# A graph-attention layer on one core: the first head's weights on SyncE's queue, and one step of transposes moved

## The chip, the cores and the metric

The kernel runs on one core of a Trainium2 chip. A core has five engines that run side by side, each through its own list of instructions in order: TensorE (PE; its weight loads are listed apart as PEld), VectorE (DVE), ScalarE (ACT), GpSimd (POOL) and SyncE (SP), which here only issues transfers. They wait for each other by semaphores. Transfers between the chip's memory and the core's are issued by SyncE, ScalarE or GpSimd into a queue of that engine, and 16 DMA engines carry them out.

The metric is the device time of one execution in microseconds (us). Times of single instructions come from the trace of one profiled execution and count from its start.

## The reference, cut to what matters

The input x has 128 graphs of 64 nodes with 512 features; all graphs share one adjacency matrix. Everything is 32-bit floating point.

```python
h = relu(layernorm(x))
# four heads, each with its own W (512x512) and a (2x512)
Wh   = einsum('bnf,hfo->bhno', h, W_heads)
f1, f2 = Wh @ a[:, :512], Wh @ a[:, 512:]
e    = leaky_relu(f1[..., :, None] + f2[..., None, :], 0.01)
attn = softmax(where(adj > 0, e, -1e9))
h    = elu(attn @ Wh)                # heads side by side: 2048 features
# the same once more with W_out (2048x512) and a_out, one head
out  = elu(gat(h, W_out, a_out))
y    = relu(out @ w1 + b1) @ w2 + b2 + out
return x + layernorm(y) * gamma + beta
```

## The kernel before, in words

The 8192 rows of x are 64 tiles of 128 rows (two graphs each), and four tiles make a group `g`; there are 16 groups. The large products are done by a scheme with seven products of half-size blocks instead of eight (`unit`, L242), so the kernel also makes sums of weight blocks: `weight_sums` (L193) makes them on GpSimd and writes them to memory as `tc`, and `piece` (L211) loads a block of weights or of such sums as a tile `w` over SyncE's queue whenever one of 11 places becomes free.

The steps are written out in the order in which they are to be issued. A scheduler then places each instruction in the list of its engine, and a tile's place is reused as soon as its last reader is done. `behind(ins, after, ...)` (L86) adds a wait of one instruction for another by hand.

**The start** (L97 to L201 and L856 to L881) is different from the rest. The first four tiles of x are loaded by `load` (L104) on SyncE's queue. ScalarE loads the vectors `a` into `ar`, a tile that VectorE cleared before (`zeros`, L113). `fetch` (L163) loads the weights of a head, 512x512, as `pw`: head 0 on ScalarE's queue, behind `zeros`; heads 1 to 3 on SyncE's queue, the later matrices on GpSimd's. Then:

- `norm1` (L339) normalizes a tile: statistics on VectorE (L326, L330, L332), the reciprocal root and bias on GpSimd (L334, L344), relu with scale and bias on ScalarE (L346), which gives `hn`. For the first four tiles the GpSimd parts are chained one behind the other.
- `transpose_h` (L359) turns `hn` on PE (`pth`, L362); ScalarE copies it to `hT`.
- `spread_a` (L171) spreads the vectors `a` of a head over 128 rows by two matmuls on PE (`pab`, L177). `fold` (L183) multiplies the head's weights by them and sums, eight instructions on VectorE per head (`jk`, L188), 32 for the four heads; the results `wa` go into `project_f` (`pf`, L372), from which the scores come.
- `head_w(m, j)` (L626) is the product of tile j with head m's weights on PE (`hw`, L629); ScalarE copies it out (L632). In the list of PE the first of them stands behind the spreads of heads 0 and 1 and the transposes of tile 0.
- `weight_sums(0)` on GpSimd (L200 to L205) reads `pw` of head 0 behind the last bias of the four tiles.

Group 0's first layer is done in this way; from group 1 on `attend1` and `project1` do it in the other order with the blocks of seven products.

**The step at group 0's second layer** (L973 to L997). `project2(0)` is a list of 28 products of blocks (`g_b`, L305: seven products of four parts each). Between its steps stands a table by step number with other work: at 15 to 21 the transposes, scores and softmax of group 2 (`softmax`, L414, whose result is the tile `s1A`, L443 and L448), at 25 `turns[1]` and at 27 `turns[4]`. Each of these two is `transpose_weights` (L473) for a pair of tiles: eight transposes on PE into two banks (`s1pt`, L485), and two copies on ScalarE to `at` (L489). The banks come from a pool of two; `s1A` has one place, so the softmax of the second pair writes its result there after the first pair's transposes have read it. The steps of the next `project1` follow.

Of the kernel before, what the change touches and what calls it, by code (L numbers as in the profile page):

```python
# [9 lines left out]
FP = mybir.dt.float32  # L10
# [12 lines left out]
def gat_preln_kernel(  # L23
# [30 lines left out]
    nc = tc.nc  # L54
    P = 128
    B, N, F = x.shape
    H = W_heads.shape[0]
# [6 lines left out]
    G = 4  # L64
# [4 lines left out]
    xf = x.rearrange("b n f -> (b n) f")  # L69
    of = out.rearrange("b n f -> (b n) f")  # L70
# [4 lines left out]
    wk = ctx.enter_context(tc.tile_pool(name="wk", bufs=2))  # L75
# [10 lines left out]
    def behind(ins, after, reason):  # L86
        tc.add_manual_dep(
            ins.ins, after.ins.name,
            mybir.DependencyInfo(mybir.DependencyClass.Sync, mybir.DependencyReason.DATA),
            reason=reason,  # L90
        )
# [9 lines left out]

    X, HN, HNS, AT = {}, {}, {}, {}

    def load(t, name="x"):  # L104

        tl = wk.tile([P, F], FP, tag="x", name=f"{name}{t}", bufs=4)
        nc.sync.dma_start(out=tl, in_=xf[ts(t, P), :])
        return tl

    X[0] = load(0)  # L110
# [1 line left out]
    ar = wk.tile([P, O], FP, tag="elu", name="ar", bufs=3)  # L112
    zeros = nc.vector.memset(ar, 0.0)  # L113
    nc.scalar.dma_start(out=ar[0:2 * H], in_=a_heads.rearrange("h (r p) -> (h r) p", p=O))
    for t in range(1, G):
        X[t] = load(t)
    aj = const.tile([P, N], mybir.dt.int32, name="aj")
    for b in range(NB):
        nc.gpsimd.dma_start(out=aj[ts(b, N), :], in_=adj)
# [42 lines left out]

    def fetch(m, after=None):  # L163
        MT[m] = big.tile([P, KC, O], FP, tag=homes[m], name=f"pw{m}")
        queue = nc.scalar if m == 0 else nc.sync if m < H else nc.gpsimd
        ins = queue.dma_start(out=MT[m], in_=mats[m].rearrange("(k p) o -> p k o", p=P))
        if after is not None:
            behind(ins, after, "not in front of what is needed first")
        return ins
# [59 lines left out]
    def flush_late():  # L229
        while late:  # L230
            late.pop(0)()

    def run(steps, side=()):

        side, done = list(side), 0
        for i, fn in enumerate(steps):
            fn()
            while done * len(steps) < (i + 1) * len(side):
                side[done]()
                done += 1  # L240
# [229 lines left out]
    def attn_weights(p):  # L470
        A1[p] = softmax(E1.pop(p), None, 2 * H, "s1", p)
# [23 lines left out]
    def stage_a(g):  # L495


        if g >= NG:
            return [], [], []
        p, r = 2 * g, 2 * g + 1  # L500

        def norms(p):
            norm1(2 * p)
            norm1(2 * p + 1)
            if p >= 2:
                ahead = 2 * p + (4 if p < 4 else 2)
                prefetch(ahead)
                prefetch(ahead + 1)

        def transposes(p):  # L510
            transpose_h(2 * p)
            transpose_h(2 * p + 1)

        return (
            [lambda: norms(p), lambda: norms(r)],
            [
                lambda: transposes(p), lambda: transposes(r), nothing, lambda: project_f(g), nothing,
                lambda: (scores1(g), attn_weights(p)), nothing, lambda: attn_weights(r),
            ],
            [nothing, lambda: transpose_weights(p), nothing, nothing, lambda: transpose_weights(r)],  # L520
        )
# [66 lines left out]
    def project1(g, h):  # L588


        z = ZB[g]
        if h == 0:
            new_h1(g)
        sums = {6: 0, 7: 1, 3: 2}
        blk = {1: "11", 2: "12", 4: "22", 5: "S1"}

        def post(what, a, b=None, to=None):
            if what[0] != "c":
                return
            nm = {"c11": "11", "c12": "12", "c21": "S1", "c22": "22"}[what]  # L600
            dst = H1[nm][:, h]
            if b is not None:
                nc.vector.tensor_tensor(to, a, b, ALU.add)  # L603
                a = to
            elu(flat(dst), flat(a), f"{what}_{g}_{h}")
            if what == "c21":
                nc.gpsimd.tensor_tensor(dst, dst, H1["22"][:, h], ALU.add)  # L607

        s = unit(
            f"a{g}_{h}", product_t(h, lambda p: ZSUM[h][sums[p]] if p in sums else z[blk[p]][:, h]),  # L610
            post, (1, 5, 6, 2, 3, 7, 4),
        )

        def next_sums():
            if h + 1 < H:
                z_sums(g, h + 1)

        return [
            s[0], lambda: (s[1](), flush_late()), lambda: (s[2](), next_sums()), s[3], s[4],
            lambda: (s[5](), late.append(s[6])),  # L620
        ]
# [84 lines left out]
    def scores2(g, j):  # L706
        if j == 0:
            F2[g] = sm.tile([P, 2, G], FP, tag="f2", name=f"f2_{g}")
        f = F2[g]
        for c in range(2):  # L710
            junk = wk.tile([P, FO], FP, tag="elu", name=f"jf{g}_{j}_{c}", bufs=3)
            nc.vector.scalar_tensor_tensor(
                junk, WH2[g][:, j], 1.0, ao[:, c, :], ALU.mult, ALU.mult,
                accum_out=f[:, c, j:j + 1],
            )
# [45 lines left out]
    def stage_e(g):  # L761

        gap = [lambda: None]
        score = [lambda j=j: scores2(g, j) for j in range(G)]
        attend = [lambda q=q: attend2(g, q) for q in range(2)]
        return (
            gap + score + [lambda: spread2(g)] + gap * 2 + [lambda: softmax2(g)] + gap * 5
            + [lambda: transpose_weights2(g)] + gap * 2 + attend[0:1] + gap * 2 + attend[1:2] + gap * 4
        )
# [83 lines left out]
        return [fn for _, _, fn in sorted(keyed, key=lambda k: k[:2])]  # L853


    for m in range(H):  # L856
        fetch(m, zeros if m == 0 else None)
    nc.vector.memset(wa, 0.0)
    norm1(0)
    ab = spread_a(0)  # L860
# [6 lines left out]
    norms, scores, turns = stage_a(1)  # L867
# [77 lines left out]
    for g in range(NG):  # L945
        if g >= 1:
            side = stage_e(g - 1)
            done, n = 0, 6 * H
            for i in range(n):
                if i % 6 == 0:  # L950
                    steps = project1(g, i // 6)
                steps[i % 6]()
                while done * n < (i + 1) * len(side):
                    side[done]()
                    done += 1
            flush_late()
        attn = attend1(g + 1) if g + 1 < NG else []
        norms, scores, turns = stage_a(g + 2)
        tr, ff, fin = feed_forward(g - 1) if g >= 1 else ([], [], [])
        if g == NG - 1:  # L960
            run(project2(g), tr + [nothing] * 6 + ff[:2])
            run(ff[2:], [
                lambda: [scores2(g, j) for j in range(G)], lambda: spread2(g), nothing, nothing,
                lambda: softmax2(g), *[nothing] * 7, lambda: transpose_weights2(g), nothing,
                *[lambda q=q: attend2(g, q) for q in range(2)], nothing,
            ])
            continue
        early = [lambda: z_sums(g + 1, 0)] if g else []
        first = mix(attn, tr, [nothing] * len(attn))
        if g >= 1:  # L970
            first[5:5] = norms[:1]
            first[10:10] = norms[1:]
        if g == 0:  # L973
            side = {
                0: lambda: (attend0(2, 1), turn0(1, 1), project_f(1)),
                1: lambda: (attend0(3, 1), turn0(2, 1)),
                2: lambda: (turn0(3, 1), scores1(1), attn_weights(2), attn_weights(3)),
                5: lambda: weight_sums(M1, LAST["pe"]),
                7: turns1[1],
                8: lambda: fetch(M2, LAST["pe"]),  # L980
                9: attn[0],
                10: lambda: (attn[1](), norms[0](), turns1[4]()),
                12: attn[2],
                13: lambda: (attn[3](), norms[1]()),
                15: scores[0],
                16: scores[1],
                17: lambda: weight_sums(M2, LAST["pe"]),
                18: scores[3],
                20: scores[5],
                21: scores[7],  # L990
                22: lambda: z_sums(g + 1, 0),
                25: turns[1],
                27: lambda: (turns[4](), load_rows()),
            }
            for i, fn in enumerate(project2(g)):
                fn()
                side.get(i, nothing)()  # L997
        else:
            run(project2(g), first + mix(
                ff[:7] + early + ff[7:12] + fin[:1] + ff[12:13] + fin[1:2] + ff[13:],  # L1000
                scores + [nothing] * 8,
            ) + mix(fin[2:], [nothing] + turns + [nothing] * 2))
# [32 lines left out]
```

## Time and profile before

| | |
|---|---|
| median of 4 runs | 2296.99 us |
| the runs | 2297.03, 2296.76, 2297.91, 2296.95 us |
| the profiled execution's own time | 2297.03 us |
| its span, first to last instruction | 2295.0 us |
| mean granted clock of TensorE | 0.998 |
| DMA, mean over the span | 157 GB/s, 361.15 MB |

How to read the lines. A row of the timeline has the start in us, the length in us, the engine, the line of the kernel, the operation, the tile written and the tiles read, the shape and a count; the brackets at the end give the idle time of the engine just before and what ended it. SPq, ACTq and POOLq are the instructions of an engine that issue transfers; their length is that of the issue, not of the transfer. A list of waits has total, number and longest. A row for a stretch of time has, from the left, its bounds and length, the busy time of PE, PEld, DVE, ACT and POOL with the number of instructions, TensorE's granted clock, the share of the DMA engines and GB/s. Matmuls overlap: one starts before the one ahead of it has ended, and their ends are modelled. Tile numbers are left out of names, so `pw` and `hw` stand for all heads.

### The profile page before, as it was taken

How to read it: one execution, taken by the hardware profiler on the slowest of the kernel's cores; microseconds unless marked ns; L12 is line 12 of the kernel's file. 1: busy time of each engine (PE TensorE's matmuls, PEld its weight loads, DVE VectorE, ACT ScalarE, POOL GpSimd, SP SyncE). 2: the span in 40 equal slices, each digit the busy share in tenths (PEclk: the TensorE clock that was granted, in tenths of full speed). 3: DMA queues.
4: the chain of work that ended last, by engine and by line, in shares of the span. 5: the costliest groups of instructions: out<-in, count | busy, mean ns of one | idle time of the engine just before them, and what ended most of it. 6: DMA issues, size and time to landing. Idle time of an engine off the chain costs nothing. (4 is left out here: it accounts for less than half of the span.)

```text
span 2295.0 us, 33254 instructions
## 1 busy us (share of the span) xinstructions
PE 2274.6 (99%) x11856; PEld 1890.7 (82%) x11856; DVE 1275.1 (56%) x2227; ACT 904.4 (39%) x1633; POOL 1018.9 (44%) x906
## 2 busy tenths in 40 slices
PE   9999999999999999999999999999999999999997
PEld 4688888888888888888888888888888888888885
DVE  7555554755546555564655546555465554744427
ACT  3535244252542525335253352534425244251512
POOL 7653524444254442634425344353443525533324
PEclk9999999999999999999999999999999999999999
DMA  7553453534545444453544545345354453635443
GB/s 284 194 183 131 147 179 133 182 131 145 176 134 184 137 151 163 136 184 131 165 152 138 184 133 178 130 147 179 132 181 133 143 178 132 183 118 168 162 147 106
DMA packets 255012, 361.15 MB, mean 157 GB/s; under 512 B 23768, under 2 KB 143608, under 8 KB 254848
## 3 DMA queue, kind: packets, MB, share of 16 engines
q1 hardware_dynamic: 249568, 340.88, 46.1%
q0 software_dynamic: 4576, 16.81, 2.0%
q8 instruction: 96, 1.57, 0.3%
q10 hardware_dynamic: 704, 1.33, 0.2%
q14 instruction: 68, 0.56, 0.1%
HBM read 331.66 MB, written 27.26 MB: 156 GB/s over the span
## 5 line engine op out<-in xcount | busy, mean ns | idle before, releaser
L305 PE MATMUL g_b<-w,h 128*128 128x256 f32 x2560 | 593.1, 379 | 0.0
L305 PEld LDWEIGHTS g_b<-w,h 128*128 128x128 f32 x2560 | 481.1, 190 | 64.6 <-issue 2.0
L289 PE MATMUL g_a<-z,w 128*128 128x256 f32 x1440 | 341.7, 380 | 0.0
L289 PE MATMUL g_a<-zs_z,w 128*128 128x256 f32 x1440 | 336.0, 381 | 0.0
L289 PEld LDWEIGHTS g_a<-zs_z,w 128*128 128x128 f32 x1440 | 269.9, 190 | 59.2 <-issue 24.3
L289 PEld LDWEIGHTS g_a<-z,w 128*128 128x128 f32 x1440 | 272.3, 190 | 41.3 <-DVE g_a L603 5.0
L607 POOL TENSOR_TENSOR hS<-hS,h 128x512 f32<-128x512 f32 x60 | 78.1, 1302 | 360.6 <-DVE hS L573 360.6
L305 PE MATMUL g_b<-w,hS 128*128 128x256 f32 x1024 | 238.2, 379 | 0.0
L305 PEld LDWEIGHTS g_b<-w,hS 128*128 128x128 f32 x1024 | 192.1, 190 | 25.0 <-issue 0.2
L571 ACT ACTIVATE exc<-g_a 128x512 f32<-128x512 f32 x240 | 142.5, 594 | 164.9 <-DVE g_a L603 97.1
L573 DVE SCALAR_TENSOR_TENSOR h<-exc,g_a 128x512 f32<-128x512 f32 x180 | 123.5, 686 | 140.8 <-ACT exc L572 140.2
L572 ACT ACTIVATE exc<-exc 128x512 f32<-128x512 f32 x240 | 151.4, 631 | 6.6
L688 POOL TENSOR_TENSOR h<-h,h 128x512 f32<-128x512 f32 x64 | 86.8, 1365 | 138.6 <-PE g_b L305 138.6
L688 POOL TENSOR_TENSOR h<-hS,h 128x512 f32<-128x512 f32 x64 | 81.5, 1275 | 145.6 <-PE g_b L305 145.3
L314 POOL TENSOR_TENSOR zs_z<-zS,z 128x512 f32<-128x512 f32 x60 | 85.2, 1420 | 136.1 <-PE g_a L289 132.9
L489 ACT COPY at<-s1pt 128x512 f32<-128x512 f32 x64 | 34.4, 589 | 268.8 <-PE s1pt L485 268.8
L833 POOL TENSOR_TENSOR xr<-xr,bs 128x512 f32<-128x512 f32 x64 | 97.5, 1528 | 77.2 <-DMA xr<-in_x_dram 41.3
L305 PE MATMUL g_d<-w,rt 128*128 128x256 f32 x512 | 121.8, 380 | 2.2 <-DVE o L825 1.0
L289 PE MATMUL g_c<-ot,w 128*128 128x256 f32 x512 | 122.7, 382 | 0.6 <-DVE ot L792 0.6
L289 PE MATMUL g_a<-zS,w 128*128 128x256 f32 x480 | 113.4, 379 | 0.0
L305 PEld LDWEIGHTS g_d<-w,rt 128*128 128x128 f32 x512 | 96.9, 190 | 17.3 <-DVE o L825 2.2
L289 PEld LDWEIGHTS g_c<-ot,w 128*128 128x128 f32 x512 | 94.9, 190 | 18.2 <-issue 5.0
(164 smaller groups left out, 3536.0 us busy)
## 6 DMA issues: line engine op xcount, KB each, us to landing
w<-tc SPq DMA_DIRECT2D x624, 256.0 KB, 2.6
w<-in_L_gnn_W_out_dram SPq DMA_DIRECT2D x192, 256.0 KB, 2.7
w<-in_L_gnn_W_heads_dram SPq DMA_DIRECT2D x180, 256.0 KB, 2.9
w<-in_L_gnn_w_dram SPq DMA_DIRECT2D x96, 256.0 KB, 2.7
x<-in_x_dram SPq DMA_DIRECT2D x64, 256.0 KB, 3.2
xr<-in_x_dram SPq DMA_DIRECT2D x128, 128.0 KB, 2.7
out_dram<-o SPq DMA_DIRECT2D x126, 128.0 KB, 2.4
tc<-pt POOLq DMA_DIRECT2D x20, 512.0 KB, 4.3
```

The source lines that it names most:

```text
L289: LAST["pe"] = nc.tensor.matmul(bk[:, o, :], w[:, k, ts(o, P)], a[:, k, :], start=start and o == 0 and k == 0, stop=k == 1, skip_group_che ...
L305: LAST["pe"] = nc.tensor.matmul(bk[:, j, :], a[:, k, ts(j, P)], w[:, k, :], start=start and n == 0, stop=i == len(ms) - 1 and k == 1, skip ...
L314: eng.tensor_tensor(s2, s1, a11, ALU.subtract)
L489: nc.scalar.copy(AT[t].rearrange("p b h n -> p (b h) n"), pt)
L571: nc.scalar.activation(ex, src, AF.Relu, scale=-1.0)
L572: nc.scalar.activation(ex, ex, AF.Exp, scale=-1.0)
L573: nc.vector.scalar_tensor_tensor(dst, ex, -1.0, src, ALU.add, ALU.max)
L607: nc.gpsimd.tensor_tensor(dst, dst, H1["22"][:, h], ALU.add)
L688: nc.gpsimd.tensor_tensor(dst[:, h], x0[:, h], x1[:, h], ALU.subtract)
L833: nc.gpsimd.tensor_tensor(xr, xr, bs, ALU.add)
```

## The change

It has two parts.

1. `fetch(0)` goes to SyncE's queue, behind `zeros` as before, and is written ahead of the loads of tiles 1 to 3 of x, which now wait for `zeros` too. SyncE's list begins with x0, pw of head 0, x1, x2, x3, pw of heads 1, 2, 3. ScalarE's queue has only `ar` at the start. On VectorE the small instruction L332 of tile 0 now stands ahead of the statistics of tile 1, where it stood behind them; two others of tiles 2 and 3 change places. The later loads of x5 to x7 come ahead of the first block of W_out on SyncE's queue.
2. `turns[1]` moves from step 25 to step 26 of the table: in PE's list four matmuls of `project2(0)` come ahead of its eight transposes, and no other order changes.

```diff
-    def load(t, name="x"):
+    def load(t, after=None):
 
-        tl = wk.tile([P, F], FP, tag="x", name=f"{name}{t}", bufs=4)
-        nc.sync.dma_start(out=tl, in_=xf[ts(t, P), :])
+        tl = wk.tile([P, F], FP, tag="x", name=f"x{t}", bufs=4)
+        ins = nc.sync.dma_start(out=tl, in_=xf[ts(t, P), :])
+        if after is not None:
+            behind(ins, after, "not in front of what is needed first")
         return tl
...
-    for t in range(1, G):
-        X[t] = load(t)
...
-        queue = nc.scalar if m == 0 else nc.sync if m < H else nc.gpsimd
+        queue = nc.sync if m < H else nc.gpsimd
...
-    for m in range(H):
-        fetch(m, zeros if m == 0 else None)
+    fetch(0, zeros)
+    for t in range(1, G):
+        X[t] = load(t, after=zeros)
+    for m in range(1, H):
+        fetch(m)
...
-                25: turns[1],
+                26: turns[1],
```

## The prediction

> **What bounds the kernel now.** I read the page first: busy shares, then TensorE's own list of waits, then the timeline of the two places that the change touches. The page says which engine sets the time.
>
> ```profile
> PE 2274.6 (99%) x11856; PEld 1890.7 (82%) x11856; DVE 1275.1 (56%) x2227; ACT 904.4 (39%) x1633; POOL 1018.9 (44%) x906
> ```
>
> TensorE (PE) is busy for 2274.6 of 2295.0 us. The other engines have half their time free, so the end is set by the work of PE, which the change leaves alone, and by its idle time, 20.4 us in all. The list of PE's waits over the whole span says what is in that:
>
> ```profile
> PE pab L177 <- DVE n1st L326: 4.3, 1, 4.3
> PE g_c L289 <- ACT t_c L255: 1.1, 1, 1.1
> ...
> PE hw L629 <- DMA pw<-in_L_gnn_W_heads_dram: 0.9, 1, 0.9
> ...
> PE s1pt L485 <- DVE s1A L443: 0.4, 1, 0.4
> ```
>
> The columns are the total, the number and the longest. Two of them lie where the change works: 0.9 us for the first head's weights (pw), and 0.4 us at the transposes of attention weights (s1pt). No other wait stands between 12 us and 300 us, so a microsecond won on PE at the start is still there at the end: the long tail follows PE. The change can win about 1.3 us by these two rows and no more, 0.06% of the time. A difference of under 0.2% (4.6 us) is what I call no change here; about that much a measurement of this kernel can tell.
>
> **Part 1, the first head's weights.** In order of time, PE at the start (start, length, engine, line):
>
> ```profile
> 4.30 3.75 PE L177 MATMUL pab<-ar,ident 128*128 128x512 f32 x4 [4.30 <-DVE n1st L326]
> 7.85 1.06 PE L362 MATMUL pth<-ident,hn 128*128 128x128 f32 x4
> 8.70 2.68 PE L177 MATMUL pab<-ar,ident 128*128 128x512 f32 x4
> 12.25 3.67 PE L629 MATMUL hw<-pw,hT 128*128 128x512 f32 x8 [0.87 <-DMA pw<-in_L_gnn_W_heads_dram]
> ...
> 17.92 3.60 PE L629 MATMUL hw<-pw,hT 128*128 128x512 f32 x8
> ```
>
> PE finishes the second spread of `a` and waits for pw until 12.25. The last of those matmuls starts at 10.79. Undisturbed ones of this shape follow each other every (3.60 - 0.59) / 7 = 0.43 us (the group at 17.92, less one matmul's own 0.59), so the product could have started at 10.79 + 0.43 = 11.22. It starts 1.03 later, and its group takes 3.67 where the undisturbed one takes 3.60: another 0.07 for starting from a standstill. The wait costs 1.03 + 0.07 = 1.10 us, a little more than the 0.87 that the row names. It goes entirely if pw lands before 11.2.
>
> When does it land? Today it is issued by ScalarE at 2.04 and lands 10.1 us later, at 12.15. The queues at that time:
>
> ```profile
> 0.73 1.81 SPq L107 DMA_DIRECT2D x<-in_x_dram  x4
> ...
> 2.04 0.44 ACTq L166 DMA_DIRECT2D pw<-in_L_gnn_W_heads_dram  x1
> ...
> 2.58 2.24 SPq L166 DMA_DIRECT2D pw<-in_L_gnn_W_heads_dram  x3
> ```
>
> By the trace's times to landing the four tiles of x arrive at 3.5, 4.2, 7.6 and 8.9 us: x2 and x3 slow down as soon as pw runs beside them, and pw shares the 16 engines with x and then with the second head's weights, which land at 13.2. In the changed order everything is on SyncE's queue: x0, pw, x1, x2, x3, then heads 1 to 3. What counts is how many bytes lie ahead. The stretches of the trace give the rate (the last column is GB/s):
>
> ```profile
> 2.00:7.00 5.00, 2.70 (x4) 1.18 (x4) 1.68 (x6) 2.10 (x2) 1.67 (x5) 1.00 0.88 285
> 2.00:9.00 7.00, 4.70 (x9) 2.51 (x10) 2.45 (x9) 2.15 (x3) 2.16 (x6) 1.00 0.91 296
> ```
>
> x0 and pw are 0.26 + 1.05 MB, with the small `ar` and `aj` 1.36 MB: at 285 GB/s that is 4.8 us from 2.0, so 6.8, and with the slowest of the engines lagging I take 7.5. The bounds are 3.5 (not before x0, which is ahead of it) and 12.15 (no sooner than today). 7.5 is near neither, but it has 3.7 us to spare before 11.2, so the term is taken whole: **-1.1 us**.
>
> The Trainium skill, "DMA: Bandwidth & Descriptors", section "Issuing engines are not separate DMA queues", says that queues of several issuing engines run on the same 16 DMA engines and interleave, so that a second issuer saves only issue time. By it the change loses no bandwidth and pw simply moves ahead of x1 to x3; the sum would be the same. The same skill speaks against it in "Perfetto Trace Analysis", section "DMA Optimizations": where issuing itself is the bottleneck, spread it over several engines; this change does the reverse. Weighed by the rows: an issue costs SyncE 1.81 / 4 = 0.45 us, so x1 to x3 are issued one such step (about 0.5 for pw, and 0.2 for its wait) later. By that rule the sum would shrink only if x1 to x3 came too late, which is the next point.
>
> **What the moved load pushes back.** pw now waits for the clearing of `ar` (VectorE, 0.90 to 1.38); x1 to x3 and heads 1 to 3 stand behind it on SyncE. x1 to x3 also have 1 MB more ahead of them: x0 to x3, pw and the small ones are 2.15 MB, at 296 GB/s 7.3 us from 2.0, so x3 lands at about 9.3 instead of 8.9, or 10 with the later issue. Who waits for it? VectorE takes the statistics of x1 to x3 ahead of the first fold, in both kernels:
>
> ```profile
> 8.98 0.69 DVE L326 BATCH_NORM_STATS2 n1st<-x 128x6 f32<-128x512 f32 x1 [0.62 <-DMA x<-in_x_dram]
> ...
> 12.22 0.69 DVE L188 SCALAR_TENSOR_TENSOR jk<-pw,pab 128x512 f32<-128x512 f32 x1 [2.00 <-DMA pw<-in_L_gnn_W_heads_dram]
> ```
>
> From the landing of x3 to VectorE being free for the fold it is 10.22 - 8.93 = 1.3 us. With x3 at 10 the fold starts at 11.3 instead of 12.22: VectorE gains 0.9 us as well. Its 32 folds end 19.5 us later (12.22 to 31.7), and PE needs the last of them at 34.34 today (pf, L372), so at 33.2 after. This holds while x3 lands before 33.2 - 19.5 - 1.3 = 12.4. ScalarE's copy of the first product stands behind hn3, which ends 3.9 us after x3's landing (12.87 against 8.93); PE wants that copy at about 17, which gives nearly the same bound. GpSimd starts its weight sums behind x3's bias, 12.02 today, so perhaps 0.5 to 1 us later; it has 1.5 us idle at 35 and its last sums for W_out reach SyncE at 88.4, some 15 us before PE reads them (from 104). So the term is **0**, covered by 2.4 us; the far bound is in the rival below.
>
> On the gain side there is nothing more ahead of 11.2: the order on PE is unchanged, the first spread waits for `ar`, whose load stays on ScalarE's queue, and x0 stays first. VectorE's eps instruction for x0 is now ahead of x1's statistics and hn0 may be 0.5 us earlier, but the transposes of hn0 follow the spread matmuls without a gap, so that gives nothing.
>
> The cold start is another thing that could blur this: PE's matmuls of 128x512 follow each other every 0.85 us until about 10 and every 0.43 after it. The Trainium skill, "TensorE: Matmul & The Clock Gate", Part 1, says that the array starts at half clock and speeds up after a window of some 3.4 us that runs freely, so that the cold stretch varies from run to run. By that page alone the sum could move by an estimated 1.7 us (3.4 at half speed) either way; the measured spread of the four runs, 1.15 us, is what I use.
>
> **Part 2, the transposes a step later.** The place in the trace:
>
> ```profile
> 156.51 1.04 PE L485 MATMUL s1pt<-ident,s1A 128*128 128x128 f32 x8
> 157.38 3.62 PE L305 MATMUL g_b<-w,h 128*128 128x256 f32 x16
> 160.59 0.69 DVE L443 TENSOR_TENSOR s1A<-s1e,s1r 128x512 f32<-128x512 f32 x1
> 161.43 1.06 PE L485 MATMUL s1pt<-ident,s1A 128*128 128x128 f32 x8 [0.43 <-DVE s1A L443]
> ```
>
> The first eight transposes at 156.51 waited for nothing; the change puts four of the following matmuls (1.73 us) ahead of them. The second eight wait 0.43 us for VectorE's softmax of the second pair. Moving the first eight does not touch that: PE has the same work ahead of 161.0 in another order, and VectorE's chain (exp at 158.53, its sum at 159.57, the product at 160.59) keeps its order. It reuses the tile s1A that the first eight read, but they would end at 159.3, before 160.59. ScalarE copies the first two results at 159.06 behind the exp; they would be ready at 159.3, so the copies end at about 160.4, before PE wants the two banks again at 161.0. The cover shrinks from 0.9 to 0.6 us. So **0**. Bounds: -0.55 (the wait of 0.43 and a restart go) and +1.07 (both copies in front of the second eight); I take 0, since both rows keep their distance.
>
> **Sum.** The profiled execution took 2297.03 us (span 2295.0 and 2.03 around it), 0.04 above the median of the four runs. 2296.99 - 1.10 - 0 = **2295.9 us**.
>
> **Rivals.**
> - *Both waits go* (2295.3): as forecast, and VectorE's softmax reaches PE in time at 161, since VectorE gains as much as PE in front or is less disturbed by GpSimd (its L435 took 1.50 us there, 0.69 elsewhere). Against it: that chain starts from PE's own scores at 146.75, so both shift together. Chance 0.12.
> - *Nothing gained* (2297.0): pw lands late all the same, or PE stops a little later for what was pushed back (x3, or part 2's banks at +1.07). For it: pw's 10.1 us are long. Against it: 3.7 us to spare. Chance 0.10.
> - *Slower: SyncE's queue doesn't carry it alone.* If the one queue ran only at the rate of x2 and x3, 0.52 MB between 4.2 and 8.9, 112 GB/s, the 2.10 MB would take 18.8 us from 2.0: x3 at 20.8, fold at 22.1, end of folds at 41.6 instead of the 33.2 wanted, so PE stands 8.4 us at pf: 2295.9 + 8.4 = 2304.3. It decides from x3 landing after 12.4, a queue below 2.1 / 10.4 = 200 GB/s. Against it: x0 and x1 alone came over this queue by 4.2 us, 0.52 MB in 2.2 us, 238 GB/s. Chance 0.03.
> - *It doesn't do what it says*: the order of the changed program has pw second on SyncE and the eight transposes one product later, so I leave this out.
>
> **Numbers.** Forecast 0.75, then 0.12, 0.10 and 0.03. The range takes in the first three with the runs' spread of about 0.5 either way and part 2's +1.07: 2294.9 to 2297.5. Faster by over 0.2% (below 2292.4) no case gives: 0.01 for what I overlook. Slower by over 0.2% (above 2301.6): 0.03, and 0.01 on top; within: 0.95.
>
> **What would show it.** Right: the product hw starts at 11.2 to 11.3 and PE's list of waits has no row for pw; pw lands at 7 to 8, x3 at 9 to 10; the fold starts ahead of 12; s1pt still waits about 0.4. Wrong: a new wait of PE at hw, pf or pth between 11 and 40 us, or one at s1pt of about a microsecond, or any wait behind it that PE did not have, above all one for weights (w) on SyncE's queue.

## The result, and the profile after

The changed kernel took a median of **2295.15 us** (2293.91 to 2297.04, 41 runs), the kernel before 2297.28 us on the same chips (2295.74 to 2299.12, 61 runs): 2.1 us less, a ratio of 0.999 with a 95% interval of 0.9986 to 0.9995 (1.1 to 3.2 us less). That is inside 0.2%, inside the range, and with the sign that was forecast, but about twice the 1.1 us that the sum named. The profiled execution took 2295.51 us, with a span of 2293.5. Two of the executions behind the medians of this document, 6018.28 us of the kernel before and 8897.45 us of "softmax earlier", lie far above all others; the medians count them and move by at most 0.05 us, the ratios leave them out.

The page's row of busy times after the change: the work of TensorE (PE) is what it was, within a microsecond.

```profile
PE 2273.7 (99%) x11856; PEld 1889.8 (82%) x11856; DVE 1272.5 (55%) x2227; ACT 904.5 (39%) x1633; POOL 1017.3 (44%) x906
```

PE's own list of waits after (total, number, longest):

```profile
PE pab L177 <- DMA ar<-in_L_gnn_a_heads_dram: 3.7, 1, 3.7
PE g_c L289 <- ACT t_c L255: 1.1, 1, 1.1
...
PE hw L629 <- ACT hT L364: 0.9, 1, 0.9
...
PE s1pt L485 <- DVE s1A L443: 0.4, 1, 0.4
```

Three things are to be seen. The row of `hw` for `pw` is gone. A row of `hw` for `hT`, 0.9 us, has come. And the first row, PE's wait before its first matmul, fell from 4.3 to 3.7, which nobody had asked for. The last row, part 2's place, has not moved. (The first wait is put down to VectorE before and to `ar` after. The spread, L177, reads only `ident` and `ar`, so I read both as the wait for `ar`; the profile does not show when `ar` landed.) PE in order of time, after:

```profile
3.67 3.68 PE L177 MATMUL pab<-ar,ident 128*128 128x512 f32 x4 [3.67 <-DMA ar<-in_L_gnn_a_heads_dram]
7.20 0.60 PE L362 MATMUL pth<-ident,hn 128*128 128x128 f32 x4
7.63 1.88 PE L177 MATMUL pab<-ar,ident 128*128 128x512 f32 x4
9.35 3.60 PE L629 MATMUL hw<-pw,hT 128*128 128x512 f32 x8
...
16.20 3.70 PE L629 MATMUL hw<-pw,hT 128*128 128x512 f32 x8 [0.91 <-ACT hT L364]
```

The product of tile 0 starts at 9.35 where it started at 12.25, 2.9 us earlier; that of tile 1 starts at 16.20 where it was 17.92, only 1.7 us earlier. Of what was won, 1.2 us are given back in between. ScalarE shows to whom:

```profile
14.38 0.81 ACT L346 ACTIVATE hn<-x,n1nb,n1rs 128x512 f32<-128x512 f32 x1 [0.18 <-POOL n1nb L344]
15.10 0.56 ACT L632 COPY hw<-hw 128x512 f32<-128x512 f32 x1
15.57 0.58 ACT L364 COPY hT<-pth 128x512 f32<-128x512 f32 x1
```

ScalarE works in order: the copy of tile 1's `hT`, for which PE waits, stands behind the normalization `hn` of tile 3. The normalizations are a chain from VectorE over GpSimd to ScalarE, and the chain of tiles 1 to 3 starts with x1, which now has a megabyte more ahead of it. VectorE gets its statistics of x1 only at 9.40, and its first fold starts at 12.35, no earlier than the 12.22 of before.

```profile
9.40 0.69 DVE L326 BATCH_NORM_STATS2 n1st<-x 128x6 f32<-128x512 f32 x1 [4.64 <-DMA x<-in_x_dram]
...
10.23 0.66 DVE L326 BATCH_NORM_STATS2 n1st<-x 128x6 f32<-128x512 f32 x1
...
10.86 0.68 DVE L326 BATCH_NORM_STATS2 n1st<-x 128x6 f32<-128x512 f32 x1
...
12.35 0.69 DVE L188 SCALAR_TENSOR_TENSOR jk<-pw,pab 128x512 f32<-128x512 f32 x1
```

VectorE waits for x1 alone: its statistics of x2 and x3 follow at 10.23 and 10.86 without a wait. `hn` of tile 3 starts 14.38 - 9.40 = 4.98 us after the statistics of x1; in the other five traces with this order of loads it is 4.97 to 4.99 us, though these statistics start anywhere from 7.94 to 9.01.

`pw` itself: the answer for the transfers issued about 1.4 us (KB of one, us from issue to landing) says that it landed at 1.41 + 7.2 = 8.6, where it was 12.15.

```profile
pw<-in_L_gnn_W_heads_dram SPq DMA_DIRECT2D x1, 1024.0 KB, 7.2
```

One trace after and one before thus give three numbers for the gain: 2.9 at the first product, 1.7 at the second, 1.45 at PE's last instruction; and the median says 2.1. The experiments are about which of them is the change's. Four questions were open:

- Which part makes the gain: the weights on SyncE's queue, or the transposes?
- Is it the wait for `pw` at all, or does PE's clock, which stepped up earlier in the trace after, make the gain by chance? The matmuls of 128x512 follow each other every 0.85 us at first and every 0.43 later; the step came at 10.3 us before and at 7.2 after. What the traces show is this pace: the granted clock reads 1.00 already before the step (the stretch from 2 to 7 us in the prediction). That the slow start is a clock at half speed is inferred; experiment 3 has a row that supports it.
- Does the order against x1 to x3 matter, or only the queue?
- Where does the earlier start of PE come from?

### The profile page after: what moved, and what is told of

It reads as the page before. It is cut to its first block, busy times and chain, and to the rows that moved or that the text cites. A ratio compares the mean times of both kernels' runs of the same rounds, so it can differ in the third digit from the quotient of the medians.

```text
span 2293.5 us, 33256 instructions
## 1 busy us (share of the span) xinstructions
PE 2273.7 (99%) x11856; PEld 1889.8 (82%) x11856; DVE 1272.5 (55%) x2227; ACT 904.5 (39%) x1633; POOL 1017.3 (44%) x906
## 3 DMA queue, kind: packets, MB, share of 16 engines
q8 instruction: 95, 1.56, 0.3%
```

## The experiments

Experiments 1 and 2, 3 and 4, and 5 make three sets, each with its own runs of the kernel before as the base: 2297.48 us (33 runs), 2297.65 (33) and 2297.43 (27). The 95% interval of a single experiment is about 2 us to either side, as much as the gain itself; so where kernels are told apart below, it is by their medians and by what the traces show, not by the intervals.

**1. Part 1 alone, part 2 alone.** Part 1 alone is the changed kernel with one line back; part 2 alone is the kernel before with that line changed.

```diff
 part 1 alone, from the changed kernel
-                26: turns[1],
+                25: turns[1],
 part 2 alone, from the kernel before
-                25: turns[1],
+                26: turns[1],
```

> The changed kernel with part 2 undone: the new order of the first loads, the transposes at step 25 again. Theory A (the loads are everything: PE's wait for the first head's weights, pw, goes; what limits the gain is a new wait of 0.9 us for hT1, which stands on ScalarE behind hn3, because x1 to x3 land only at 9.4 to 10.8): the same time as the changed kernel, 2.1 us below the kernel before (1.5 by the two profiles), and s1pt still waits 0.4 us. Theory B (part 2 carries some of it): 0.4 us or more slower than the changed kernel, so at most 1.7 below the kernel before.

> The kernel before with part 2 alone (transposes at step 26). Theory A: no difference (within 0.3 us), hw starts at 12.2 after waiting for pw, s1pt waits 0.4 us. Theory B: 0.4 us or more faster.

Part 1 alone: **2295.34** us, ratio 0.999 (0.9981 to 1.0). Part 2 alone: **2297.36**, ratio 0.9999 (0.999 to 1.0008). By the medians the gain is part 1's, and part 2 is worth 0.1 us or less. PE at the start of part 1 alone:

```profile
3.78 3.75 PE L177 MATMUL pab<-ar,ident 128*128 128x512 f32 x4 [3.78 <-DMA ar<-in_L_gnn_a_heads_dram]
...
10.36 3.60 PE L629 MATMUL hw<-pw,hT 128*128 128x512 f32 x8
...
15.95 3.60 PE L629 MATMUL hw<-pw,hT 128*128 128x512 f32 x8
```

and of part 2 alone, which has the start of the kernel before:

```profile
4.51 3.75 PE L177 MATMUL pab<-ar,ident 128*128 128x512 f32 x4 [4.51 <-DVE n1mv L330]
...
8.91 1.91 PE L177 MATMUL pab<-ar,ident 128*128 128x512 f32 x4
12.44 3.67 PE L629 MATMUL hw<-pw,hT 128*128 128x512 f32 x8 [1.63 <-DMA pw<-in_L_gnn_W_heads_dram]
18.11 3.60 PE L629 MATMUL hw<-pw,hT 128*128 128x512 f32 x8
```

Here the clock stepped up earlier (8.9 us) than in the trace of before, PE had its spreads done sooner, and then waited longer: 1.63 us, though `pw` landed only 0.2 us later (12.3, it was 12.1). So the 0.87 of the first trace was a low draw of that wait. Part 1 alone has neither the wait for `pw` nor the new one for `hT`; its second product starts at 15.95, 2 us ahead of before.

**2. The order against x1 to x3.** Head 0's weights stay on SyncE's queue, but all of x goes ahead of them, or x1 alone.

```diff
 all of x first
-    fetch(0, zeros)
     for t in range(1, G):
-        X[t] = load(t, after=zeros)
+        X[t] = load(t)
+    fetch(0, zeros)
 x1 first
+    X[1] = load(1)
     fetch(0, zeros)
-    for t in range(1, G):
+    for t in range(2, G):
```

> The changed kernel with pw of head 0 on SyncE's queue behind all four tiles of x, which do not wait for the clearing. Theory A: x lands at about 3.5, 4.2, 5.3 and 6.3 us, pw at 9.3 (2.15 MB at 296 GB/s); PE waits for pw until 9.5 if its matmuls are at full pace by then, for nothing if not; no wait for hT1; hw of tile 1 starts 5.7 us after hw of tile 0, so at 15.2 to 16.9 where the changed kernel has 16.2: 1.0 to 2.7 us below the kernel before. Rival C (the gain is the clock: PE's matmuls came to full pace at 7.2 us in the changed kernel's profile and at 10.4 in the one before, and the loads matter little): whatever the order of loads, a gain only in those profiles in which the pace doubles early. Rival D (one queue for everything is what counts, as ar lands 0.6 us earlier when ScalarE's queue carries it alone): PE starts at 3.7 here too; by theory A's reading of ar (it lands together with the tile issued ahead of it) PE starts at 4.2 or later, since x1 is issued ahead of ar again.

> The changed kernel with pw behind x0 and x1 and ahead of x2 and x3. Theory A: x1 lands at 4.2, pw at about 8.5, x2 and x3 at 9.5 to 10.5. hn1 is early, but hT1's copy still stands behind hn3 on ScalarE, so hw of tile 1 starts at about 15.5 to 16.2: equal to the changed kernel or up to 0.7 faster, 2.1 to 2.8 below the kernel before. If instead the late x1 itself were the cause of the wait for hT1, the wait of 0.9 us goes and the time is 0.9 below the changed kernel. PE starts at 4.2 by theory A's reading of ar, at 3.7 by rival D.

All of x first: **2295.5** us, ratio 0.9991 (0.9982 to 1.0); x1 first: **2296.59**, 0.9995 (0.9986 to 1.0003). With all of x first, PE's start is

```profile
4.57 3.60 PE L177 MATMUL pab<-ar,ident 128*128 128x512 f32 x4 [4.57 <-DVE n1mv L330]
...
10.16 3.60 PE L629 MATMUL hw<-pw,hT 128*128 128x512 f32 x8
...
15.75 3.60 PE L629 MATMUL hw<-pw,hT 128*128 128x512 f32 x8
```

No wait for `pw` here either: issued about 2.6, it landed 6.9 us later, at 9.5, and VectorE folds at 9.61. So the words "ahead of the other three" are not what gains; the queue is. On ScalarE's queue, with the same x0 to x3 ahead of it and issued half a microsecond earlier, `pw` took 10.1 us. In all four traces of the old order it took 10.1 to 10.7, in the three with all of x first on SyncE's queue 6.9 to 7.9. I read the difference as what it shares the 16 engines with: on a queue of its own it runs beside heads 1 to 3, in SyncE's queue they come behind it. No run held heads 1 to 3 back alone, so this reason is argued, not shown. The Trainium skill, "DMA: Bandwidth & Descriptors", section "Issuing engines are not separate DMA queues", says that transfers of all issuing engines interleave on the same 16 engines; the 10.1 against 6.9 us agree.

x1 first fell short of the theory. Its front is as early as the others' (second product at 16.08), but the median is only 0.9 us below before, and its trace loses 0.8 us much later, near 1920 us, where PE waits for group 13. GpSimd in that trace:

```profile
1914.26 1.27 POOL L833 TENSOR_TENSOR xr<-xr,bs 128x512 f32<-128x512 f32 x1 [1.14 <-DMA xr<-in_x_dram]
...
1916.02 1.27 POOL L833 TENSOR_TENSOR xr<-xr,bs 128x512 f32<-128x512 f32 x1 [0.49 <-DMA xr<-in_x_dram]
```

A load of the residual rows `xr` comes late, GpSimd stops for it in order, and the normalization, the copy and then PE stand behind. Measured against the trace of before, the same spot costs PE 0 to 0.5 us in ten of the other traces and 0.8 in two, with no pattern by kernel that I found. One of these two is the kernel with x held (experiment 4), whose median is 1.88 us below before all the same; so this spot alone does not account for the missing microsecond, and both its cause and that of the missing time stay open. It blurs the end of every span by up to 0.8 us, and so I read the front from the front.

**3. Is it the clock?** If the early step of the clock made the gain, then warming PE in the kernel before would make it too. Six matmuls of zeros, whose results nobody reads, are put on PE at 1.58 us, before it has other work.

```diff
     nc.vector.memset(wa, 0.0)
+    wf, junkb = wa.rearrange("p k c -> p (k c)"), flat(bank("warm"))
+    for i in range(6):
+        nc.tensor.matmul(junkb[:, 0:P], wf, wf, start=True, stop=True)
```

> The kernel before with six more 128x128 matmuls at the very start of PE, on the cleared tile wa, whose results nobody reads: PE is busy from about 1.6 us and its matmuls reach full pace one to three microseconds sooner. Theory A (in the kernel before pw's landing at 12.2 sets the first product, whatever PE's pace): PE is ready by 9 to 10 us, its wait for pw grows from 0.9 to 2.2 or more, hw still starts at 12.2 to 12.5, and the time is unchanged within 0.3 us. Rival C (the clock step is the gain): hw starts sooner by the time won, the kernel gains 1 us or more.

The kernel before with this: **2298.77** us, ratio 1.0004 (0.9995 to 1.0013), not faster. PE:

```profile
1.58 2.93 PE L861 MATMUL warm<-wa 128*128 128x128 f32 x12 [1.58 <-DVE wa L858]
...
7.55 1.88 PE L177 MATMUL pab<-ar,ident 128*128 128x512 f32 x4
12.87 5.20 PE L629 MATMUL hw<-pw,hT 128*128 128x512 f32 x8 [3.44 <-DMA pw<-in_L_gnn_W_heads_dram]
...
20.07 3.60 PE L629 MATMUL hw<-pw,hT 128*128 128x512 f32 x8
```

The clock steps up at 5.7 us and the spreads are done by 9.4, yet the product starts at 12.87, no earlier than in the other traces of the old order (12.25 to 12.68): `pw` is the gate, and time won ahead of it becomes a wait, now 3.44 us. That refutes the clock as the cause. The other side of it is in "softmax earlier" of experiment 4: its step came at about 10 us, nearly as late as before, and its second product still starts at 16.34, 1.6 us ahead. And here the early step turns a profit into a loss, where the expectation had no change: after this wait the eight matmuls take 5.20 us instead of 3.60. The row by stretches of that trace (the granted clock is third from the end) says why:

```profile
10.00:13.00 3.00, 0.13 (x1) 0.16 (x1) 0.87 (x6) 2.00 (x3) 1.88 (x6) 0.92 1.05 398
13.00:16.00 3.00, 3.00 (x4) 1.35 (x5) 3.00 (x11) 0.44 (x1) 3.00 (x3) 0.51 1.05 386
16.00:19.00 3.00, 3.00 (x11) 1.53 (x10) 3.00 (x11) 0.89 (x2) 3.00 (x3) 1.00 1.06 380
```

The clock is taken back to half: 0.5 us of it in the first stretch (0.92 of 3 us) and 2.9 in the second (0.51), some 3.4 us together; it began to fall at about 12.5, some 3.1 us after PE's last matmul had ended (8.84 + 0.59). At 0.51 the matmuls follow each other every 0.85 us (13.86, 14.71, 15.56), which is the pace of the start; that is the support for reading the slow start as half clock. The runs of this kernel lie between 2296.72 and 2300.39 us, those of its base between 2296.73 and 2298.31, so the fall may not come in every execution. The Trainium skill, "TensorE: Matmul & The Clock Gate", section "HAM oscillation — how this bites in real kernels", says that an idle time of some 3.4 us sends the array back to half clock; the wait of 3.44 us here, with the fall 3.1 us into it, agrees to a few tenths, and so do the other traces, whose waits of up to 1.63 us at this place cost no clock.

**4. What else the new front allows.** Three kernels from the changed one: its softmax of the second pair one step earlier, so that the wait at `s1pt` can go; all of x first but held behind `zeros`; and both.

```diff
 softmax earlier
-                17: lambda: weight_sums(M2, LAST["pe"]),
-                18: scores[3],
-                20: scores[5],
-                21: scores[7],
+                17: lambda: (weight_sums(M2, LAST["pe"]), scores[3]()),
+                19: scores[5],
+                20: scores[7],
 all of x first, held
-    fetch(0, zeros)
     for t in range(1, G):
         X[t] = load(t, after=zeros)
+    fetch(0, zeros)
```

> The changed kernel with group 2's scores and both softmaxes one step (1.7 us) earlier in the table of project2(0): steps 17, 19 and 20 for 18, 20 and 21. Theory A (the wait of 0.44 us at s1pt is set by VectorE's chain from the scores, so part 2 could not touch it): the wait goes, 0.4 to 0.6 us below the changed kernel. If the wait is set by something else (banks, ScalarE), it stays.

> As the run with x first and then pw on SyncE's queue, but x1 to x3 wait for the clearing of ar, so that x1 is issued at 1.41 instead of 1.2. Theory E (ar, issued by ScalarE at 1.42, lands together with the tile that SyncE issued ahead of it, since with x1 ahead it landed at 4.3 to 4.6 and without at 3.7): PE starts at 3.7 to 3.8, pw lands at 9.7 to 9.9, no wait for hT1; hw of tile 1 at 15.3 to 16.7 by the clock step; 0 to 0.8 us below the run with x first without the wait. If ar's landing depends on what lies beside it on the engines instead, PE starts at 4.3 or later as there.

> The two together: x first, held behind the clearing, then pw, and the early softmax. Theory A: the sum of the two, about 0.5 us below the run before it, 2.6 to 3.2 below the kernel before, PE's list of waits without rows for pw, hT1 and s1pt.

Softmax earlier: **2295.03** us, ratio 0.9988 (0.9979 to 0.9997). All of x first, held: **2295.77**, 0.9992 (0.9984 to 1.0001). Both: **2295.21**, 0.999 (0.9981 to 0.9999), 2.4 us below its base where 2.6 to 3.2 were expected. In the last of them the transposes at `s1pt` wait for nothing any more:

```profile
156.55 1.04 PE L485 MATMUL s1pt<-ident,s1A 128*128 128x128 f32 x8
157.63 0.69 DVE L443 TENSOR_TENSOR s1A<-s1e,s1r 128x512 f32<-128x512 f32 x1 [0.67 <-PE s1pt L485]
159.16 1.04 PE L485 MATMUL s1pt<-ident,s1A 128*128 128x128 f32 x8
```

VectorE's result `s1A` now comes at 157.63 + 0.69, ahead of PE's need. In the trace of the softmax alone PE's lead over before grows from 1.56 to 2.19 us at this place. By times it is worth 2295.77 - 2295.21 = 0.6 us on one base; so the wait of 0.43 and its restart could be had, but by moving VectorE's work and not PE's transposes. The kernel with x held has this start:

```profile
3.83 3.75 PE L177 MATMUL pab<-ar,ident 128*128 128x512 f32 x4 [3.83 <-DMA ar<-in_L_gnn_a_heads_dram]
...
10.77 3.67 PE L629 MATMUL hw<-pw,hT 128*128 128x512 f32 x8 [0.81 <-DMA pw<-in_L_gnn_W_heads_dram]
```

PE begins 0.7 us earlier than with all of x first and not held, and then waits 0.81 us for `pw`, so the time is no better: 1.88 us below its base, where the one not held is 1.98 below its own. That made a new theory: `ar`, only 16 KB, is late when x1 has been issued before it. I read it from every trace whose PE starts on `ar`. With x1 issued by about 1.2 us, PE starts at 4.30, 4.45, 4.51, 4.57 and 4.56 (mean 4.48); with x1 at 1.4 or later at 3.67, 3.74, 3.78, 3.83, 4.16 and 4.31 (mean 3.92). The means differ by 0.56 us, but the groups overlap at 4.30 and 4.31; 3.83 and 4.31 come from the same order of loads (x held, and both), 3.67 and 4.16 from the very same program; and no kernel moved `ar` alone. The tendency is seen; its cause is not settled.

**5. Warm-up where `pw` is no gate, the changed kernel and the one before once more.** The six matmuls of experiment 3 in the changed kernel, then with the earlier softmax as well; beside them the two kernels unaltered.

> The changed kernel with the six early matmuls on the cleared tile. Theory A: pw lands at 7.5 to 8.7, so PE, at full pace from 5 to 7, has no long wait: the first product starts at 8.7 to 9.4 and the clock does not fall back, unlike in the kernel before with the same matmuls (wait of 3.4 us, then half pace from 12.5 to 16.0). The second product (tile 1) is then held by hT1 behind hn3 on ScalarE, at 15.0 to 16.2. 0 to 0.7 us below the changed kernel. If early matmuls harm as such, it is 1 us or more above it.

> The run before it with the early softmax as well: 0.5 us less again by the wait at s1pt, 0.5 to 1.2 below the changed kernel, the fastest of all if theory A's terms add up.

> The changed kernel unaltered, for a second trace of its start and its time beside the others. Theory A: ar at 3.6 to 3.9, first product at 9.3 to 11 by the clock step, second product at 15.9 to 16.4 either way; 1.6 to 2.2 us below the kernel before.

> The kernel before unaltered, for a third trace of its start. Theory A: ar at 4.3 to 4.6, the first product at 12.2 to 12.9 after a wait for pw whose length follows from the clock step (0.9 in the first trace with the step at 10.3, 1.6 with the step at 8.9), the second product at 17.9 to 18.5 either way.

| kernel, third set | median us | ratio to before (95%) |
|---|---|---|
| changed, unaltered | 2295.19 | 0.9989 (0.998 to 0.9998) |
| changed, warm | 2294.42 | 0.9987 (0.9979 to 0.9996) |
| changed, warm, softmax earlier | **2293.86** | 0.9985 (0.9977 to 0.9994) |

The kernel before once more, for its trace alone, took 2299.24 us in that one run; its span, 2295.8, is much like the other two of the old front (2295.0 and 2295.5). The last row of the table has the lowest median of all, 3.6 us below before and 1.3 below the changed kernel of the same set; the intervals of the three overlap, so the order among them rests on the medians; the spans of the two warm traces, 2292.3 and 2292.6 with the earlier softmax, do not repeat it. The earlier softmax is again worth 0.56 us. The warm-up is worth 0.8 us here and lost 1.1 in the kernel before: the same instructions, with and without a gate behind them. PE in the warm kernel:

```profile
8.85 3.60 PE L629 MATMUL hw<-pw,hT 128*128 128x512 f32 x8
...
15.23 3.70 PE L629 MATMUL hw<-pw,hT 128*128 128x512 f32 x8 [0.63 <-ACT hT L364]
```

PE is now as early as the chain from the statistics of x1 (8.44 in this trace) over `hn` of tile 3 (13.41) to the copy lets it be, and waits for `hT` again. The two unaltered kernels repeat what the first traces showed, but for the changed one's first spread, which was expected at 3.6 to 3.9 and came at 4.16; the kernel before

```profile
4.45 3.75 PE L177 MATMUL pab<-ar,ident 128*128 128x512 f32 x4 [4.45 <-DVE n1mv L330]
...
8.85 2.25 PE L177 MATMUL pab<-ar,ident 128*128 128x512 f32 x4
12.68 3.67 PE L629 MATMUL hw<-pw,hT 128*128 128x512 f32 x8 [1.58 <-DMA pw<-in_L_gnn_W_heads_dram]
18.34 3.60 PE L629 MATMUL hw<-pw,hT 128*128 128x512 f32 x8
```

and the changed one

```profile
4.16 3.75 PE L177 MATMUL pab<-ar,ident 128*128 128x512 f32 x4 [4.16 <-DMA ar<-in_L_gnn_a_heads_dram]
...
10.47 3.60 PE L629 MATMUL hw<-pw,hT 128*128 128x512 f32 x8
...
16.06 3.60 PE L629 MATMUL hw<-pw,hT 128*128 128x512 f32 x8
```

## Why the prediction was right, and where its size was off

With three traces of the old front (before, part 2 alone, before again) and four of the new (after, part 1 alone, softmax earlier, after again) the front can be read as means:

| us | old front | new front |
|---|---|---|
| first spread of `a` on PE | 4.42 | 3.84 |
| PE could start tile 0's product (last spread + 0.43) | 10.94 | 10.23 |
| tile 0's product starts | 12.46 | 10.23 |
| tile 1's product starts | 18.12 | 16.14 |

The difference in the last row, **1.98 us**, lies beside 2.1 us by the medians. It is the row to read because what is won there stays: in the trace after, PE is 1.61 us ahead at `pf` (34.34 and 32.73) and 1.59 behind the second `s1pt` (162.33 and 160.74). And it varies by only 0.4 us in either group, where tile 0's product moves by 1.4 in the new one: an early step of the pace is cut off in the old front by the landing of `pw`, in the trace after by `hT`.

The direction and the cause were right. That the time also lies inside the range is partly luck: it is 0.25 us above the lower end, 2294.9, and the value named nearest to it, 2295.3, belongs to the rival "both waits go", which did not come, since `s1pt` still waits 0.4 us. The product also starts earlier than the sign given for it, 11.2 to 11.3, in all four traces of the new front.

1. **"The wait costs 1.03 + 0.07 = 1.10 us" was mis-sized, and this is the step that failed.** The mechanism held: the wait is gone in all four traces. But by the prediction's own measure it was 12.25 - 11.22 = 1.03 in the first trace, 12.44 - 10.66 = 1.78 in part 2 alone and 12.68 - 10.94 = 1.74 in before again: 1.5 on the mean, and the only trace at hand had the lowest. A wait is the difference of two events, and both of them move: the landing from 12.15 to 12.5, PE being ready, with the step of the pace (8.9 to 10.3 us), from 10.66 to 11.22. The first trace had the earliest landing and the latest PE. The prediction set its estimate of 1.7 us for the cold start aside for the spread of the totals, 1.15 us. Totals do not tell how far a single wait moves: their standard deviation is 0.57 us over the 61 runs before and 0.65 over the 41 after, where PE waits for `pw` in none of the four traces.
2. **"On the gain side there is nothing more ahead of 11.2" fell.** PE starts 0.58 us earlier on the mean, presumably because `ar` arrives earlier, and the prediction had taken its landing as given because its queue was not touched. With the step of the pace, which came a little earlier too, PE is ready for the product 0.7 us earlier.
3. **"What the moved load pushes back ... 0"** held for the median and not for the single trace. x3 was to land at 9.3 to 10 and came at 10.7, 9.4, 9.3 and 10.3 in the four traces. But the chain was reckoned from the wrong tile: it starts with x1, which landed at 4.2 before and at 9.4, 8.0, 7.9 and 9.0 now, and VectorE reaches x2 and x3 after they have landed. The fold was to start at 11.3 and started 2.95 us after the statistics of x1, at 12.35, 11.00, 10.89 and 11.96; so VectorE's gain of 0.9 came in full in two of four. It cost nothing at `pf`: in the trace after the folds end at 31.9 against 31.8 before and PE, at `pf` at 32.73, does not wait. The second bound, ScalarE's copy behind hn3, was put at "nearly the same" distance, for a PE that wants it at 17; with PE earlier it binds in one trace of four, a wait of 0.91 us, with which tile 1's product starts 6.85 us behind tile 0's instead of 5.59, so 0.3 on the mean. A new wait at `hw` is what the prediction had named as a sign of being wrong, and the rival that let PE stop a little later for what was pushed back was true in part.
4. **pw at 7.5** came at 8.6, 7.3, 7.2 and 8.3, 7.9 on the mean. The 3.7 us to spare carried that; with PE ready at 9.35 in the trace after, 0.75 were left.
5. **Part 2 at 0** held: part 2 alone is 0.1 us from before, and the changed kernel and part 1 alone are both 2.1 below their bases. The row at `s1pt` reads 0.44 after and 0.43 before, and the reason given, that VectorE's chain sets it, is shown by experiment 4.
6. **The queue that doesn't carry it** did not come: no wait at `pf`, and the stretch from 2 to 9 us ran at 303 GB/s where it was 296.

The sum with the measured terms, as book-keeping of means: 1.5 for the wait, 0.07 for the restart, 0.7 for PE being ready earlier, less 0.3 for `hT`, 2.0 us. What is open: why `ar` is earlier, the late loads of `xr` near 1920 us, and why x1 first gains a microsecond less than the others.

## What to carry to other kernels

A wait for a transfer is the difference of two events, and where both vary from run to run, one trace gives one draw: take two or three traces of the kernel before, and work the wait out from the range of each event; the spread of the total times does not give it. When a load is moved back, look for the first of the chain that it feeds, not only for the last. Order transfers by need in one queue before spreading them over several, since what lies on another queue shares the engines with what is wanted first. And warm PE, or make anything early, only after the gate behind it is gone.

## What the runs showed of the hardware that was not expected

- In a wait of 3.44 us PE's granted clock fell, after some 3.1 us, to 0.51 for 3.4 us, which cost 5.20 - 3.60 = 1.6 us on the product behind it; waits up to 1.63 us there did not.
- The granted clock reads 1.00 in the stretch from 2 to 7 us, though the matmuls there follow each other every 0.85 us, the pace that goes with 0.51 after that wait.
- A megabyte on ScalarE's queue, beside three more on SyncE's, took 10.1 to 10.7 us to land; in SyncE's queue ahead of those three 6.9 to 7.9, with the same x0 to x3 ahead and though issued later.
- A transfer of 16 KB let PE begin at 4.48 us on the mean where a tile of 256 KB had been issued before it on another queue, and at 3.92 where that tile was issued later; the groups overlap, and the cause was not separated.
